# Expert weights stored as pieces of 128 rows of 2 KB instead of rows of 8 KB, in a gated cross-attention and mixture-of-experts kernel

## The chip, the core and the metric

The kernel runs on one core of one Trainium2 chip. A core has TensorE (PE in the profile, with its weight loads as PEld), VectorE (DVE), ScalarE (ACT), GpSimd (POOL) and SyncE (SP). SP computes nothing here: it issues DMAs, in the order of its program, and waits before each for what that DMA needs. POOL issues the indirect DMAs (gathers and scatters). All DMAs are carried out by the core's 16 DMA engines; those that SP issues appear in the profile as queue q1, those of POOL as q0, those of ACT as q10.

The metric is device time in microseconds, lower is better. The kernel before takes 445.69 us, the median of five runs from 444.35 to 446.97.

## The reference, cut to what matters

```python
x = x + jnp.tanh(g_xattn[0]) * xattn(layernorm(x), ctx_1024, itok, Wq, Wkv, Wo)
x = x + jnp.tanh(g_ffn[0])   * ffn(layernorm(x), gate_w, w1, b1, w2, b2)

# ffn: 8 experts, the best 2 per token
gate_probs = softmax(einsum('bsh,eh->bse', x, gate_w))
top_v, top_i = jax.lax.top_k(gate_probs, 2)
comb_w = einsum('bsk,bske->bse', top_v, one_hot(top_i, 8))
for e in range(8):
    h = silu(einsum('bsh,hf->bsf', x, w1[e]) + b1[e])     # w1[e]: 256 x 1024
    y = einsum('bsf,fh->bsh', h, w2[e]) + b2[e]           # w2[e]: 1024 x 256
    out = out + y * comb_w[..., e:e+1]
```

There are 4 x 512 = 2048 tokens of 256 channels, all in fp32. In the attention each token looks at four neighbouring rows of a key and value table (16 heads of 16); which rows is given by `itok`. One expert's `w1` is 1 MB, its `w2` too.

## The kernel before, in words

**Attention and routing.** The 2048 tokens are 16 tiles of 128. The key and value table is projected first and written to DRAM (`near`). For each tile POOL gathers its four table rows per token (L224, 1 MB), DVE does the scores and the weighted sum (L391 to L432), and PE the projections. Then tiles are routed in groups: DVE finds each token's two best experts and the place of the token in the expert's region of a DRAM table `xs`, and POOL scatters the normalised rows there (L331, two scatters for each tile). `queue` turns the counts so far into a list `blk` of blocks, each of 128 rows of one expert. The list is lengthened as tiles are done, and at the end eight scatters of a padding row (`xs<-padrow,pad`) fill the last rows.

**Blocks of the experts.** There are 39 of them. For block `s`, `fetch` lets SP read the expert's number and the block's first row into registers and issue five DMAs in this order: `w1s` (the expert's whole `w1`, 1 MB, L693), `xg` (the 128 rows, L697, which waits for the scatters that may write them), `b1s` (L699), `ms` (L702), `b2s` (L708). PE then turns the rows (`turn`, L714), multiplies them with `w1` (`up`, 32 matmuls, L729, with silu on ACT), and, one block later, with `w2` (`down`, 16 matmuls, L754). In PE's order: `up(s)`, `turn(s+1)`, `down(s-1)`. DVE forms the weighted result `yw` (L764), and POOL adds it into the output with an indirect accumulating DMA (L765).

**What sets the order.** Most buffers of a block are threefold (`ffn` pool). `b2s` of a block waits until DVE's `yw` three blocks earlier has read the old one; since SP goes in program order, the next block's `w1s` and `xg` are issued only after that. `w2` of all experts is loaded once: eight loads of 1 MB (L851), two behind each of the first four attention tiles.

**How the weights lie.** On the host, `by_row` puts each expert's weights in the order in which the partitions of SBUF want them: row `e*128 + p` of `w1` or `w2` is the 8 KB that partition `p` holds of expert `e`. So a load is 128 rows, each contiguous in DRAM and in SBUF:

```python
nc.sync.dma_start(
    out=w1s.rearrange("p k f -> p (k f)"), in_=w1[bass.ds(be_v * P, P), :]
)
```

Of the kernel before, what the change touches and what calls it, by code (L numbers as in the profile page):

```python
# [15 lines left out]

P = 128
KW = 4
EPS = 1e-5
FMAX = 3.4028234663852886e38  # L20

# [2 lines left out]
def gated_xattn_moe(  # L24
# [25 lines left out]
    nc = tc.nc  # L50
    NTOK, D = x.shape
    E = b2.shape[0]
    F = b1.shape[1] * P
    NT = NTOK // P
    KD = D // P
    NF = F // P
# [4 lines left out]
    GROUPS = [(sum(sizes[:i]), n) for i, n in enumerate(sizes)]  # L61
    EDGE = KW - 1
    LKW = LKV + 2 * EDGE
# [8 lines left out]
    @contextmanager  # L72
    def in_order():

        traced = nc.cur_bb.bb.instructions
        old = {i.name for i in traced}
        yield
        for i in nc.cur_bb.bb.instructions:
            if i.name not in old and i.engine == mybir.EngineType.DVE:
                if order:  # L80
                    tc.add_manual_dep(i, order[-1].name, ORDER, reason="in this order")
                order.append(i)
# [3 lines left out]
    def surely(tiles):  # L86

        return max(0, -((E * (P - 1) - TOPK * P * tiles) // P))
# [31 lines left out]
    for b in range(1, B):  # L120
        nc.sync.dma_start(
            out=src_rest[:, :, b - 1, :], in_=kvT[:, :, b * LKW + EDGE : b * LKW + EDGE + P]
        )
    gw_sb = const.tile([P, KD, E], F32, name="gw_sb")
    w2_sb = const.tile([P, E * NF, D], F32, name="w2_sb")
# [11 lines left out]
        out=upto,  # L137
        in_=all_one,
# [44 lines left out]
    nc.vector.tensor_copy(seg_f, seg_i)  # L183
    neg = const.tile([P, NT, KW], F32, name="neg")
    for o in range(KW):
        nc.vector.tensor_scalar(
            neg[:, :, KW - 1 - o], seg_f, float(o), -FMAX, ALU.is_lt, ALU.mult
        )
# [25 lines left out]
    def project_near(kv, psum, src, b, after=None):  # L214
        copy = nc.vector.tensor_copy if b == 0 else nc.scalar.copy
        project(kv, psum, src, P, near[b], EDGE, f"near{b}", copy, after)
        return nc.sync.dma_start(
            out=near[b][0:EDGE, :].unsqueeze(0),
            in_=kv[0:1, :].unsqueeze(1).to_broadcast([1, EDGE, 2 * D]),
        ).ins  # L220
# [23 lines left out]
    def rsqrt(pool, mv, rs, nm, n, name):  # L244
# [3 lines left out]
        g = nc.vector  # L248
        g.tensor_scalar(v, mv[:, :, 1], EPS, None, ALU.add)
        g.tensor_scalar(  # L250
# [48 lines left out]
    def layers(is_near):  # L299
        order.clear()  # L300
        with ExitStack() as inner:
            _layers(inner, is_near)

    def _layers(ctx, is_near):
# [36 lines left out]
        def reads_rows(i, done):  # L341

            for other in scatters[:done]:
                tc.add_manual_dep(i, other.name, SYNC, reason="rows of any scatter so far")
            for other in scatters[done:]:
                tc.declare_no_dep(i, other, reason="rows of their own")
            reads.append(i)
# [5 lines left out]
        def rows_of(t):  # L353
            gt = gat.tile([P, KW, 2 * D], F32, tag="g", name=f"g_{t}")
            if is_near:
                gather_near(gt, t)
            else:
                gather(gt, every, B * LKW, idx_every[:, t : t + 1])
            gathered[t] = gt
# [4 lines left out]
        def stage_in(t):  # L364

            xn = att.tile([P, D], F32, tag="xn", name=f"xn_{t}")
            normalise(xn, t, rsa[:, t : t + 1], nma[:, t : t + 1])
            px = ps_m.tile([P, KD, P], F32, tag="m", name=f"px_{t}")
            for k in range(KD):
                nc.tensor.transpose(px[:, k, :], xn[:, ts(k, P)], ident)  # L370
            xnT = att.tile([P, KD, P], F32, tag="xnT", name=f"xnT_{t}")
            nc.scalar.copy(xnT, px)
            ops[t] = xnT

        def stage_ask(t):

            xnT = ops.pop(t)
            pq = ps_q.tile([P, D], F32, tag="q", name=f"pq_{t}")
            for k in range(KD):
                nc.tensor.matmul(  # L380
                    pq, xnT[:, k, :], wq_sb[:, k, :], start=(k == 0), stop=(k == KD - 1)
                )
            ops[t] = pq

        def stage_attend(t):

            pq = ops.pop(t)
            gt = gathered.pop(t)
            prod = att.tile([P, KW, D], F32, tag="prod", name=f"prod_{t}")
            sc = small.tile([P, KW, H], F32, tag="sc", name=f"sc_{t}")  # L390
# [79 lines left out]
        def centre():  # L470
            pg = ps_m.tile([P, E], F32, tag="m", name="pg")
            for k in range(KD):
                nc.tensor.matmul(pg, all_one, gw_sb[:, k, :], start=(k == 0), stop=(k == KD - 1))
            nc.vector.scalar_tensor_tensor(
                gwc,
                pg.unsqueeze(1).to_broadcast([P, KD, E]),
                -1.0 / D,
                gw_sb,
                ALU.mult,
                ALU.add,  # L480
            )
# [195 lines left out]
        def fetch(s, blk, i):  # L677
            be_v = nc.values_load(  # L678
                blk[0:1, i, 0:1],
                engines=[SP],  # L680
                min_val=0,
                max_val=E - 1,
                skip_runtime_bounds_check_because=why,
            )
            br_v = nc.values_load(  # L685
                blk[0:1, i, 1:2],
                engines=[SP],
                min_val=0,
                max_val=E * CAP,
                skip_runtime_bounds_check_because=why,  # L690
            )
            w1s = ffn.tile([P, KD, F], F32, tag="w1s", name=f"w1s_{s}")
            nc.sync.dma_start(  # L693
                out=w1s.rearrange("p k f -> p (k f)"), in_=w1[bass.ds(be_v * P, P), :]
            )
            xg = ffn.tile([P, D], F32, tag="xg", name=f"xg_{s}")
            reads_rows(nc.sync.dma_start(out=xg, in_=xs[bass.ds(br_v, P), 0:D]).ins, done[s][0])  # L697
            b1s = ffn.tile([P, NF], F32, tag="b1s", name=f"b1s_{s}")
            nc.sync.dma_start(out=b1s, in_=b1[bass.ds(be_v * P, P), :])  # L699
            ms = ffn.tile([P, 2], F32, tag="ms", name=f"ms_{s}", bufs=6)  # L700
            reads_rows(
                nc.sync.dma_start(  # L702
                    out=ms, in_=xs[bass.ds(br_v, P), bass.ds(be_v * 2 + D, 2)]
                ).ins,
                done[s][0],
            )
            b2s = ffn.tile([P, D], F32, tag="b2s", name=f"b2s_{s}")
            nc.sync.dma_start(out=b2s, in_=b2[bass.ds(be_v, 1), :].to_broadcast([P, D]))  # L708
            return w1s, xg, b1s, ms, b2s
# [102 lines left out]
        for i in range(NT + 1):  # L812
            if i + AHEAD < NT:
                rows_of(i + AHEAD)
            if i + 1 < NT and i:
                stage_in(i + 1)
            attend = stage_attend(i) if i < NT else iter(())
            queued = surely(i) if i in ends else 0
            with in_order():
                if i != sizes[0] + sizes[1]:  # L820

                    next(attend, None)
                    next(attend, None)
                if i == 1:
                    centre()
                if i:
                    stage_out(i - 1)
                if i + 1 < NT:
                    stage_ask(i + 1)
                if i in ends and i > sizes[0]:  # L830
                    for _ in stage_route(ends[i]):
                        pass
                if i == NT:
                    queue(i, NS - before)
                elif queued:
                    queue(i, queued - before)
                    before = queued
                for _ in attend:
                    pass
                if i + 1 == sizes[0] + sizes[1]:  # L840
                    for _ in stage_route(0):
                        pass
            if is_near and i == 0:
                for b in range(1, B):
                    project_near(
                        kv_near[:, b, :], ps_m, src_rest[:, :, b - 1, :], b, after=exps[0]
                    )
            if i < E // 2:

                for e in (2 * i, 2 * i + 1):  # L850
                    load = nc.sync.dma_start(out=w2_sb[:, ts(e, NF), :], in_=w2[ts(e, P), :])  # L851
                    tc.add_manual_dep(load.ins, seen[i].name, SYNC, reason="after its rows")
        s = 0
        while s < NS:
# [79 lines left out]
```

## Time and profile before

| | |
|---|---|
| median of 5 runs | 445.69 us |
| the profiled execution | 447.19 us, with a span of 445.0 us in the profile |
| PE busy | 376.3 us (85% of the span) |
| DVE, ACT, POOL busy | 217.9, 174.0, 167.7 us |
| DMA | 94.76 MB in 43977 packets; q1 47.4% and q0 21.6% of 16 engines' span |
| DMAs that the change touches | `w1s` 39 of 1 MB, `w2_sb` 8 of 1 MB |

Up to some 82 us DVE does the attention of the first tiles while the gathers and the `w2` loads go on. From 82 to some 290 us the rest of the attention and the first half of the blocks share PE. From some 304 us PE has only blocks left, the last 17 of them in a steady rhythm.

How to read it: busy time alone does not tell what bounds the kernel. The lists of waits say for which engine's instruction or which DMA an engine stood idle, and for how long; the chain of work that ended last is followed back from the end. A DMA's landing time is counted from its issue to its completion as the waiting engines see it. In the DMA part, a queue's line gives packets, megabytes, and the time of its packets as a share of the 16 engines' span.

### The profile page before, as it was taken

How to read it: one execution, taken by the hardware profiler on the slowest of the kernel's cores; microseconds unless marked ns; L12 is line 12 of the kernel's file. 1: busy time of each engine (PE TensorE's matmuls, PEld its weight loads, DVE VectorE, ACT ScalarE, POOL GpSimd, SP SyncE). 2: the span in 40 equal slices, each digit the busy share in tenths (PEclk: the TensorE clock that was granted, in tenths of full speed). 3: DMA queues.
4: the chain of work that ended last, by engine and by line, in shares of the span. 5: the costliest groups of instructions: out<-in, count | busy, mean ns of one | idle time of the engine just before them, and what ended most of it. 6: DMA issues, size and time to landing. Idle time of an engine off the chain costs nothing. (4 is left out here: it accounts for less than half of the span.)

```text
span 445.0 us, 7747 instructions
## 1 busy us (share of the span) xinstructions
PE 376.3 (85%) x2311; PEld 330.9 (74%) x2311; DVE 217.9 (49%) x748; ACT 174.0 (39%) x476; POOL 167.7 (38%) x187
## 2 busy tenths in 40 slices
PE   1577755379999899599899899989999999999991
PEld 0235533268899788499889889878999999999980
DVE  1859996865987985664984954110111111111100
ACT  0322224127458467166557553323332424242320
POOL 4111124413472535323723627725342334242321
PEclk9996665569999999889999999999999999999996
DMA  6599993473976692695776966867767777786612
GB/s 204 180 355 388 423 393 131 158 251 143 300 217 234 217 292 47 223 340 160 243 195 169 257 161 187 260 176 207 235 165 230 182 212 185 210 216 181 150 16 27
DMA packets 43977, 94.76 MB, mean 213 GB/s; under 512 B 15756, under 2 KB 32524, under 8 KB 35864
## 3 DMA queue, kind: packets, MB, share of 16 engines
q1 hardware_dynamic: 33224, 65.66, 47.4%
q0 software_dynamic: 9840, 27.47, 21.6%
q10 hardware_dynamic: 864, 1.06, 0.7%
q8 instruction: 21, 0.34, 0.3%
q14 instruction: 28, 0.23, 0.2%
HBM read 80.17 MB, written 13.99 MB: 212 GB/s over the span
## 5 line engine op out<-in xcount | busy, mean ns | idle before, releaser
L729 PE MATMUL ph<-xgT,w1s 128*128 128x128 f32 x1248 | 152.1, 277 | 0.1
L729 PEld LDWEIGHTS ph<-xgT,w1s 128*128 128x128 f32 x1248 | 149.0, 193 | 2.5 <-DVE xgT L717 0.5
L754 PE MATMUL py<-w_sb,hT 128*128 x624 | 147.0, 383 | 2.0 <-DVE yw L764 0.7
L739 ACT ACTIVATE hT<-ph,b1s 128x128 f32<-128x128 f32 x312 | 88.0, 372 | 113.8 <-issue 90.0
L754 PEld LDWEIGHTS py<-w_sb,hT 128*128 128x128 f32 x624 | 114.4, 191 | 17.3 <-issue 4.1
L765 POOL DMA_INDIRECT out<-yw,ms x39 | 63.1, 1617 | 125.3 <-DMA out<-yw,ms 45.3
L763 POOL TENSOR_SCALAR b2s<-b2s,ms 128x256 f32<-128x256 f32 x39 | 42.4, 1087 | 50.1 <-DMA b2s<-in_b 49.1
L764 DVE SCALAR_TENSOR_TENSOR yw<-py,ms,b2s 128x256 f32<-128x256 f32 x39 | 18.8, 483 | 81.9 <-PE py L754 79.8
L717 DVE COPY xgT<-pxg 128x256 f32<-128x256 f32 x39 | 16.4, 420 | 86.0 <-PE pxg L714 86.0
L331 POOL DMA_INDIRECT xs<-rows,pos x32 | 33.6, 1051 | 27.3 <-DVE upb L619 6.5
L224 POOL DMA_INDIRECT g<-near,idx_near x16 | 18.1, 1131 | 50.1 <-DVE v L424 34.7
L714 PE MATMUL pxg<-ident,xg 128*128 128x128 f32 x78 | 15.7, 284 | 12.2 <-DMA xg<-xs 12.2
L380 PE MATMUL pq<-wq_sb,xnT 128*128 128x256 f32 x64 | 22.2, 479 | 3.8 <-DVE prod L391 3.8
L445 PE MATMUL po<-wo_sb,aoT 128*128 128x256 f32 x64 | 22.9, 492 | 2.8 <-ACT aoT L442 2.8
L739 ACT ACT_TABLE_LOAD x16 | 20.5, 1283 | 11.4 <-issue 9.8
L380 PEld LDWEIGHTS pq<-wq_sb,xnT 128*128 128x128 f32 x64 | 15.9, 251 | 8.9 <-DVE prod L391 4.7
L391 DVE TENSOR_TENSOR prod<-pq,g 128x1024 f32<-128x1024 f32 x16 | 19.5, 1217 | 4.9 <-PE pkv_near L206 4.9
L714 PEld LDWEIGHTS pxg<-ident,xg 128*128 128x128 f32 x78 | 9.8, 145 | 14.6 <-DMA xg<-xs 7.7
L424 DVE TENSOR_TENSOR v<-g,pr 128x1024 f32<-128x1024 f32 x16 | 19.9, 1242 | 0.5
L394 DVE TENSOR_REDUCE sc<-prod 128x64 f32<-128x1024 f32 x16 | 19.5, 1218 | 0.4
L445 PEld LDWEIGHTS po<-wo_sb,aoT 128*128 128x128 f32 x64 | 14.4, 241 | 7.0 <-ACT aoT L442 5.1
L442 ACT COPY aoT<-pa 128x256 f32<-128x256 f32 x16 | 6.0, 375 | 27.3 <-PE pa L440 27.1
(142 smaller groups left out, 314.0 us busy)
## 6 DMA issues: line engine op xcount, KB each, us to landing
w1s<-in_w SPq DMA_DIRECT2D x39, 1024.0 KB, 5.8
w_sb<-in_w SPq DMA_DIRECT2D x8, 1024.0 KB, 15.1
xg<-xs SPq DMA_DIRECT2D x39, 128.0 KB, 5.6
b2s<-in_b SPq DMA_DIRECT2D x39, 128.0 KB, 4.1
x_sb<-in_x SPq DMA_DIRECT2D x4, 512.0 KB
near<-kv_near SPq DMA_DIRECT2D x4, 256.0 KB, 3.8
out<-x_sb SPq DMA_DIRECT2D x4, 256.0 KB, 3.0
out<-x_sb SPq DMA_DIRECT2D x5, 128.0 KB
```

The source lines that it names most:

```text
L331: i = nc.gpsimd.indirect_dma_start(out=xs, out_offset=bass.IndirectOffsetOnAxis(ap=where, axis=0), in_=rows, in_offset=None,).ins
L380: nc.tensor.matmul(pq, xnT[:, k, :], wq_sb[:, k, :], start=(k == 0), stop=(k == KD - 1))
L391: seen[t] = nc.vector.tensor_tensor(prod, pq.unsqueeze(1).to_broadcast([P, KW, D]), gt[:, :, 0:D], ALU.mult).ins
L394: nc.vector.tensor_reduce(sc.rearrange("p o h -> p (o h)"), prod.rearrange("p o (h d) -> p (o h) d", d=HD), AX.X, ALU.add,)
L424: nc.vector.tensor_tensor(v.rearrange("p o (h d) -> p o h d", d=HD), gt[:, :, D : 2 * D].rearrange("p o (h d) -> p o h d", d=HD), pr.unsqu ...
L445: nc.tensor.matmul(po, aoT[:, k, :], wo_sb[:, k, :], start=(k == 0), stop=(k == KD - 1))
L714: nc.tensor.transpose(px[:, k, :], xg[:, ts(k, P)], ident)
L729: nc.tensor.matmul(ph[:, i, :], w1s[:, k, ts(f, P)], xgT[:, k, :], start=(k == 0), stop=(k == KD - 1),)
L739: nc.scalar.activation(hT[:, f, :], ph[:, i, :], AF.Silu, bias=b1s[:, f : f + 1])
L754: nc.tensor.matmul(py, hT[:, f, :], w2_sb[:, bass.ds(be_v * NF + f, 1), :].rearrange("p o d -> p (o d)"), start=(f == 0), stop=(f == NF - 1),)
L763: nc.gpsimd.tensor_scalar(b2s, b2s, ms[:, 0:1], None, ALU.mult)
L765: acc = nc.gpsimd.indirect_dma_start(out=out, out_offset=bass.IndirectOffsetOnAxis(ap=ms[:, 1:2].bitcast(I32), axis=0), in_=yw, in_offset= ...
```

## The change

Each expert's 128 rows of 8 KB are cut into four pieces: piece `c` holds the `c`-th 2 KB of each of the 128 rows, and lies in DRAM as 128 rows of 2 KB, 256 KB in all. The four pieces of an expert follow one another. A load still brings the same 1 MB to the same places in SBUF, but partition `p` now gets four separate rows of 2 KB, 256 KB apart. This holds for the 39 loads of `w1s` and the 8 of `w2_sb`. Nothing else is changed; the order of the instructions on PE, DVE, ACT, POOL and SP is the same, and so are their waits.

```diff
+PIECES = 4
...
             w1s = ffn.tile([P, KD, F], F32, tag="w1s", name=f"w1s_{s}")
             nc.sync.dma_start(
-                out=w1s.rearrange("p k f -> p (k f)"), in_=w1[bass.ds(be_v * P, P), :]
+                out=w1s.rearrange("p k (c f) -> p (k c) f", f=KD * F // PIECES),
+                in_=w1[bass.ds(be_v * (PIECES * P), PIECES * P), :].rearrange(
+                    "(c p) n -> p c n", p=P
+                ),
             )
...
-                    load = nc.sync.dma_start(out=w2_sb[:, ts(e, NF), :], in_=w2[ts(e, P), :])
+                    load = nc.sync.dma_start(
+                        out=w2_sb[:, ts(e, NF), :].rearrange(
+                            "p (c f) d -> p c (f d)", c=PIECES
+                        ),
+                        in_=w2[ts(e, PIECES * P), :].rearrange("(c p) n -> p c n", p=P),
+                    )
...
+    def in_pieces(w):
+        w = w.reshape(E, P, PIECES, -1)
+        return w.transpose(0, 2, 1, 3).reshape(E * PIECES * P, -1)
...
-        "w1": by_row(L0_ffn_w1),
+        "w1": in_pieces(by_row(L0_ffn_w1)),
...
-        "w2": by_row(L0_ffn_w2),
+        "w2": in_pieces(by_row(L0_ffn_w2)),
```

## The prediction

> **What bounds the kernel now.** I read the list of engines first, then the busy time by stretches, to see where PE has idle time at all; after that PE's waits, before and after 305 us.
>
> ```profile
> 304.00:431.00 127.00, 126.66 (x864) 118.88 (x864) 15.58 (x35) 39.25 (x138) 44.78 (x35) 1.00 0.70 185
> ```
>
> The columns are the stretch, its length, busy time of PE, PEld, DVE, ACT and POOL, the granted clock, the DMA share and GB/s. In the last stage PE is busy for 126.66 of 127 us at full clock, while the DMA engines are busy for 0.70 of the time. So the loads could be somewhat slower there at no cost, as long as each arrives in time. PE's waits from 84 to 305 us, then from 305 us to the end (us in total, times, longest):
>
> ```profile
> PE pxg L714 <- DMA xg<-xs: 12.2, 7, 5.6
> PE pa L440 <- DVE ao L432: 5.7, 5, 1.5
> ...
> PE py L754 <- DVE yw L764: 0.7, 1, 0.7
> ```
>
> PE never waits for `w1s` or `w2`, the loads that change. The DMA it waits for is `xg`, seven times, all before 305 us. Whether the change matters is therefore decided by what these loads do to other transfers: `xg` follows `w1s` in the same queue (q1), and the scatters that `xg` waits for run on q0 beside `w1s`.
>
> SP's issues in the last stage, and PE's turns:
>
> ```profile
> 309.32 0.33 SPq L693 DMA_DIRECT2D w1s<-in_w  x1
> 310.17 0.33 SPq L697 DMA_DIRECT2D xg<-xs  x1
> 315.66 0.33 SPq L708 DMA_DIRECT2D b2s<-in_b  x1
> 318.46 0.38 PE L714 MATMUL pxg<-ident,xg 128*128 128x128 f32 x2
> ```
>
> The rows asked for at 310.17 are turned at 318.46, 8.29 us later; the landing of `xg` has a median of 5.6 us. The margin is 2.7 us in each of the last 16 blocks, those fetched from 301 us on (the intervals there lie between 7.9 and 8.4). SP itself rests from 311.8 (`ms` issued) to 315.66, when `b2s` may go: 3.9 us to spare.
>
> **The change part by part.** *Time of the packets.* Two stretches give prices, one with hardly anything but `w2` in packets of 8 KB (43 to 44.5 us), and one with mostly the table writes in packets of 2 KB (33.5 to 35.5):
>
> ```profile
> q1 hardware_dynamic: 84, 0.61, 96.9%
> ...
> q1 hardware_dynamic: 347, 0.69, 91.2%
> ```
>
> The first is 0.969 x 1.5 us x 16 = 23.3 engine-us for 0.61 MB, or 38.1 ns per KB. The second is 0.912 x 2 x 16 = 29.2 for 0.69 MB, or 42.3 ns per KB, and it holds 48 packets of a few bytes too. The single packets recorded in the trace agree: the 8 KB ones have a median of 309 ns, the 256 packets of 2 KB that loads of ACT's queue brought from DRAM 84 ns. A load of 1 MB gives each engine 8 packets of 309 ns = 2.47 us now, and 32 of 84 ns = 2.69 us then: +0.22 us. Bounds: 4 x 77 ns, nothing gained or lost, below; above, the 53.8 ns per KB of q1 in the busy last stage (61.7% of 49 us for 8.99 MB), 110 ns a packet, which would be 3.5 us or +1.05 a load. That second row mixes in thousands of tiny packets, so I take +0.22.
>
> *The issue on SP.* An issue with one row per partition takes 0.33 us. The only loads with two rows per partition, `src_rest` (L121), take 0.56 to 0.61 us. Four rows cost +0.25 us if it is the extra dimension that costs, +0.75 if it is each extra row. The longest `w1s` issue now is 0.90 us (at 301.25), which shows that SP can be held back while the queue is full; 32 packets per engine fill it sooner. I take +0.25 to +0.75, and note that SP's 3.9 us of rest covers either.
>
> *The last 16 blocks.* `xg` lands later by 0.22, at worst by 1.05 + 0.75 = 1.8 us. The margin of 2.7 us covers both: nothing.
>
> *The eight `w2` loads.* 8 x 0.22 = 1.8 us more of transfer. They are issued from 27.8 to 50.5 us; the DMA engines are full until about 68.5 us, and the first use (L754) is at 101.10. Cover: 30 us. Behind them on SP stand the output stores (waiting for DVE anyway), and `w1s` of the first block at 82.65. Gathers share the engines here, but DVE never waits for a gather between 27 and 82 us. Nothing.
>
> *The seven waits for `xg`.* Three of them (at 100.30, 195.25 and 303.55 us, 0.26, 0.17 and 0.25 us long) follow a `w1s` directly, and PE has no margin: each grows by 0.22 us, or by 0.22 + 0.75 at worst where the issue shows as well. In these three the queue is still bringing `b2s` when `w1s` is issued, so the longer issue is hidden and I take 0.22: 3 x 0.22 = +0.7 us (bound 2.9).
>
> The other four (at 91.22, 185.71, 224.46 and 295.44 us; 5.56, 3.77, 0.61, 1.55) come from scatters that landed late. Their `w1s` was issued at least 6.4 us before `xg`. While it runs the scatters get nothing: from 176.4 to 179.4 us three scatters were issued, but the only queue with packets was
>
> ```profile
> q1 hardware_dynamic: 97, 0.79, 93.8%
> ```
>
> Now the scatters wait for 8 long packets per engine. If 32 short ones are served in one go as well, they wait 0.22 us longer each, +0.9 over the four. If the engines change over to q0 in between, scatters land sooner: the best is the 2.4 us that they take from 60 to 80 us, against 4.4 in the median and 7.8 for the padding at 285.18. That is worth 2.1 us at 91.22 and at 185.71 and the whole of 0.61 and 1.55: 6.4 us at most. Nothing in the trace shows which, and the two ends are far apart; the row nearest to it, the three microseconds without one scatter packet, says that a load is not interrupted. I take 0.
>
> **Sum:** +0.7 us on the profiled execution's 447.19 (span 445.0 and 2.2 around it). That execution lies 1.5 above the median of the runs, 445.69, so I add the 0.7 to the median: 446.4 us.
>
> **Two rules of the Trainium skill.** The change's own direction has a rule against it. "Perfetto Trace Analysis", DMA Optimizations, says that batching small transfers, its example being from 2 KB to 4 or 8 KB, can raise throughput dramatically. The rows above put the difference at 9 to 11%, and in stages where PE sets the pace; by the rule the loads would be the bound and the time clearly longer. On the scatters, "DMA: Bandwidth & Descriptors", Queues, rings and completion order, says that an engine goes round the queues packet by packet, where one packet may hold 9 to 17 descriptors. If 8 descriptors are such a unit, a load in 32 would be broken off one to three times, and the sum would go towards the 6.4 us gain. No row here shows how many descriptors are drained together.
>
> **The rivals.**
>
> *Faster: scatters slip in between the short packets.* For it: the scatters' landing of 4.4 us against 2.4 when no load runs. Against it: the load's bytes are the same, so what scatters gain they must take from it. Worked out: 0.7 - 6.4 = -5.7, or 440.0 us. From 180 to 210 us the mean granted clock is 0.89, after the wait of 3.77 us; if that wait shrinks so much that the clock does not fall, some 3.3 us (0.11 x 30) more.
>
> *Slower: the load takes longer than the turn allows, in each of the last blocks.* Place: `xg` behind `w1s` in q1. It decides from 2.7 us more per load, which is (2.47 + 2.7) / 32 = 161 ns for a packet of 2 KB, 1.9 times the 84. For it: packets of one partition now lie 256 KB apart, and no row shows such a read. Against it: even the mixed row gives 110. Past that point each 0.4 us costs 16 x 0.4 = 6.4 us: 452.8.
>
> *Slower by less: SP is held back when the queue is full.* `xg`, `b1s` and `ms` are then issued later in the mixed stage, where SP also issues stores and has no fixed rest. For it: the 0.90 us issue at 301.25, 0.57 over the usual. The three tight waits grow by 0.22 + 0.75 + 0.57 = 1.5 us each: +4.6, 450.3.
>
> *The loads change nothing that can be seen*, in packets or landing, since the queue could join adjacent rows: it would be the same 445.7. Rows 256 KB apart cannot be joined, so I fold this into the likeliest.
>
> **How the numbers follow.** Chances: likeliest 0.50 (own range 445.0 to 448.6, from nothing to the bound of 2.9 on the three waits), faster rival 0.20, load too slow 0.18, SP held back 0.12. The repeated runs lie within 0.3% of their median, and 0.5%, 2.2 us, is about what a measurement of this kernel can tell from no change. The likeliest gives 0.46 to within 0.5%, and 0.02 to each side. Faster: 0.20 + 0.02 = 0.22; same 0.46; slower 0.18 + 0.12 + 0.02 = 0.32. The range goes down to the faster rival at 440.0, which leaves out about half of it, and up to 452, past the held-back SP and just under the slow load's price, which leaves out about half of that: some 0.2 in all.
>
> **What the profile after would show.** Right: q1 with some 18,000 packets more (47 x 384), landing of `xg` in the last stage 5.7 to 6.5 us, still no wait for `xg` after 305 us, the three tight waits 0.2 to 0.3 longer, the `w1s` issue between 0.58 and 1.1 us. Wrong: a wait of PE for `xg` or `w1s` in the last stage, a period there above the present 7.25 us, or the waits at 91, 186 and 295 us clearly shorter or longer. The forecast fails if an order among the queues that I cannot see decides when scatters land.

## The result, and the profile after

The changed kernel takes 450.07 us against 447.3 us for the kernel before, medians of 52 and 94 runs: a ratio of 1.0060, with a 95% interval from 1.0044 to 1.0075. It is slower by 0.6%, or 2.7 us (2.0 to 3.4). The ratio leaves out the few executions that lie more than 1.5% above the fastest of their kernel. The forecast was 446.4 against 445.69, so +0.7 us; the time lies in the range. The sign of the sum was right, its size was a quarter of what came. The likeliest case of the forecast was a change within 0.5%; the ratio is just beyond that, and 0.5% lies inside its interval.

The two profiled executions do not show this difference: 447.36 us now (span 445.2), 447.19 before (445.0). One execution differs from the next of the same kernel by more than the effect, so the profile tells here what happened to single steps, and the repeated runs tell the sum.

From the DMA part of the page of the changed kernel, q1's packets, megabytes and share of 16 engines' span:

```profile
q1 hardware_dynamic: 51272, 65.66, 47.8%
```

q1 has 18,048 packets more than the 33,224 before, which is 47 x 384 exactly. They carry the same bytes, and the share of the engines' time rose only from 47.4 to 47.8%.

The busy time in the last stage (stretch, length, PE, PEld, DVE, ACT, POOL, granted clock, DMA share, GB/s):

```profile
304.00:431.00 127.00, 126.28 (x865) 118.55 (x863) 15.50 (x34) 38.88 (x136) 45.09 (x35) 1.00 0.69 184
```

PE's waits of the changed kernel from 84 to 305 us, then from 305 us to the end (us in total, times, longest):

```profile
PE pxg L718 <- DMA xg<-xs: 14.1, 7, 5.6
...
PE py L758 <- DVE yw L768: 0.7, 1, 0.7
```

PE is as busy in the last stage as it was (126.28 of 127 us), and it still waits there for no weights and no `xg`. What grew is the list's first row, `xg` before 305 us: 14.1 us in place of 12.2, again seven times. These are the seven turns (start, duration, then in brackets the idle time before), and ahead of them the three of the kernel before that the prediction called tight:

```profile
100.30 0.41 PE L714 MATMUL pxg<-ident,xg 128*128 128x128 f32 x2 [0.26 <-DMA xg<-xs]
195.25 0.44 PE L714 MATMUL pxg<-ident,xg 128*128 128x128 f32 x2 [0.17 <-DMA xg<-xs]
303.55 0.41 PE L714 MATMUL pxg<-ident,xg 128*128 128x128 f32 x2 [0.25 <-DMA xg<-xs]
...
89.93 0.69 PE L718 MATMUL pxg<-ident,xg 128*128 128x128 f32 x2 [5.63 <-DMA xg<-xs]
100.05 0.41 PE L718 MATMUL pxg<-ident,xg 128*128 128x128 f32 x2 [1.20 <-DMA xg<-xs]
185.38 0.66 PE L718 MATMUL pxg<-ident,xg 128*128 128x128 f32 x2 [3.92 <-DMA xg<-xs]
195.27 0.44 PE L718 MATMUL pxg<-ident,xg 128*128 128x128 f32 x2 [0.88 <-DMA xg<-xs]
224.39 0.44 PE L718 MATMUL pxg<-ident,xg 128*128 128x128 f32 x2 [0.51 <-DMA xg<-xs]
294.21 0.41 PE L718 MATMUL pxg<-ident,xg 128*128 128x128 f32 x2 [0.98 <-DMA xg<-xs]
303.04 0.41 PE L718 MATMUL pxg<-ident,xg 128*128 128x128 f32 x2 [1.00 <-DMA xg<-xs]
```

They are the same seven turns as before. The three tight ones (100, 195 and 303 us) went from 0.26, 0.17 and 0.25 us to 1.20, 0.88 and 1.00, together +2.4. The four behind late scatters went from 5.56, 3.77, 0.61 and 1.55 to 5.63, 3.92, 0.51 and 0.98, together -0.45. The 1.9 us do not appear in the span, mostly because the first turn came 1.3 us earlier in this execution than in the one before.

SP's issues in the last stage, and a turn:

```profile
308.82 0.38 SPq L694 DMA_DIRECT2D w1s<-in_w  x1
309.73 0.33 SPq L701 DMA_DIRECT2D xg<-xs  x1
315.15 0.33 SPq L712 DMA_DIRECT2D b2s<-in_b  x1
317.95 0.38 PE L718 MATMUL pxg<-ident,xg 128*128 128x128 f32 x2
```

The issue of the 512 packets takes 0.38 us in place of 0.33. The single packet records of the 16 loads in that stage give the time from a load's issue to the end of its last packet: 5.51 us in the median before, 5.77 now. The turns stay 7.24 to 7.25 us apart.

From 176.4 to 179.4 us two scatters were issued, at 176.40 and 178.41 (in the kernel before there were two as well, at 176.87 and 178.89; the prediction's third had begun at 175.57). All the packets that the DMA engines carried in these three microseconds:

```profile
q1 hardware_dynamic: 393, 0.80, 80.0%
```

q0 has not one, as in the same stretch of the kernel before. But that is not how loads and q0 always meet. From 190.4 to 193.9 us, while a `w1s` load runs, the packets of an output scatter (`out<-yw,ms`, rows of 1 KB on q0) come beside it in both kernels, first the kernel before, then the changed one:

```profile
q1 hardware_dynamic: 180, 1.07, 81.1%
q0 software_dynamic: 102, 0.10, 18.2%
...
q1 hardware_dynamic: 510, 0.99, 80.0%
q0 software_dynamic: 144, 0.13, 23.6%
```

And from 197 to 200 us of the changed kernel a gather (`g<-near`, rows of 8 KB on q0) runs beside the next `w1s` load, in rows of 2 KB, and takes most of the engines' time:

```profile
q0 software_dynamic: 124, 0.96, 77.1%
q1 hardware_dynamic: 153, 0.29, 25.5%
```

So a load is not always served in one go, neither in 8 packets per engine nor in 32. Taken in the order of the queue, the packet records give each load's own time. The twelfth load, issued near 190 us, takes 3.2 to 3.7 us from its first packet to its last in the four records with `w1` in rows of 8 KB and `xg` behind it (two of them from the experiments below), with 29 to 56 of the gather's 128 packets in that time. In the four with 2 KB it takes 5.3 to 5.4 us, with 111 to 124. The sixth load, which meets no q0 packet in any of the eight, takes 3.6 to 3.9 and 3.6 to 3.9 us.

What falls on the first trace is the rival in which the load gets too slow for the turn of the last stage. The rival in which scatters slip in keeps its mechanism and loses its gain: rows of q0 do pass beside the load's packets, but the four waits behind scatters lose only the 0.45 us above. The third, SP held back, would need long issues; they have a median of 0.38 us, with a longest of 0.93 against 0.90 before.

### The profile page after: what moved, and what is told of

It is laid out like the page before. It is cut to its first block, busy times and chain, and to the rows that moved or that the text cites. A ratio compares the mean times of both kernels' runs of the same rounds, so it can differ in the third digit from the quotient of the medians.

```text
span 445.2 us, 7747 instructions
## 1 busy us (share of the span) xinstructions
PE 374.8 (84%) x2311; PEld 330.0 (74%) x2311; DVE 217.8 (49%) x748; ACT 174.3 (39%) x476; POOL 166.2 (37%) x187
## 3 DMA queue, kind: packets, MB, share of 16 engines
q1 hardware_dynamic: 51272, 65.66, 47.8%
## 4 chain that ended last, share of the span: by engine, by line
PE 49%; DVE 22%; DMA 16%; issue 5%; ACT 3%; POOL 2%; SPq 2%; ACTq 0%; DVEq 0%; POOLq 0%
PE ph L733 21%; PE py L758 20%; DMA xs<-rows,pos 3%; DMA g<-near,idx_near 3%; DMA xg<-xs 3%; PE po L446 3%; DVE v L425 3%; DMA x_sb<-in_x 2%; PE pxg L718 2%; POOL xs L332 2%; DMA b2s<-in_b 1%; DVE sc L395 1%; DVE prod L392 1%; ACT hT L743 1%; DVE v L431 1%
## 5 line engine op out<-in xcount | busy, mean ns | idle before, releaser
L767 POOL TENSOR_SCALAR b2s<-b2s,ms 128x256 f32<-128x256 f32 x39 | 43.5, 1116 | 48.3 <-DMA b2s<-in_b 47.2
L718 PE MATMUL pxg<-ident,xg 128*128 128x128 f32 x78 | 15.7, 284 | 14.1 <-DMA xg<-xs 14.1
L446 PEld LDWEIGHTS po<-wo_sb,aoT 128*128 128x128 f32 x64 | 14.1, 235 | 6.8 <-ACT aoT L443 4.9
L441 PE MATMUL pa<-ident,ao 128*128 128x128 f32 x32 | 7.5, 320 | 10.8 <-DVE ao L433 10.8
```

The source lines that it names most:

```text
L446: nc.tensor.matmul(po, aoT[:, k, :], wo_sb[:, k, :], start=(k == 0), stop=(k == KD - 1))
L718: nc.tensor.transpose(px[:, k, :], xg[:, ts(k, P)], ident)
L767: nc.gpsimd.tensor_scalar(b2s, b2s, ms[:, 0:1], None, ALU.mult)
```

## The experiments

Two questions were open: which loads cost the time, and whether the waits for `xg` are the place. Theory A said that the 39 `w1` loads cost it, through `xg`, which stands behind a longer load where PE has no margin. Theory B, its rival, put it into the eight `w2` loads, in the stage in which the DMA engines are full. Theory C was any other cost of the `w1` loads, one that stays when `xg` no longer stands behind them. All ratios are to the kernel before on the same chip, with 95% intervals. The first and the third group of runs were on one chip (kernel before: 450.2 and 450.0 us), the second on another (447.6).

### One weight at a time

Only `w1` in pieces; against the changed kernel the edit puts `w2` back:

```diff
-    load = nc.sync.dma_start(out=w2_sb[...].rearrange("p (c f) d -> p c (f d)", c=PIECES), in_=...)
+    load = nc.sync.dma_start(out=w2_sb[:, ts(e, NF), :], in_=w2[ts(e, P), :])
...
-        "w2": in_pieces(by_row(L0_ffn_w2)),
+        "w2": by_row(L0_ffn_w2),
```

> Only the 39 w1 loads are in pieces, the eight w2 loads are rows of 8 KB as before. Theory A (the rows xg wait behind a longer w1 load, at three blocks without margin): the whole cost stays, ratio to the kernel before 1.004 to 1.008, and PE's waits for xg total 13.5 to 14.5 us against 12.2. Theory B (the w2 loads, in the stage where the DMA engines are full, delay the gathers or the stores): ratio 1.000 within 0.2%.

Measured: 451.72 us, 1.0031 (0.9994 to 1.0068). The waits for `xg` sum to 13.6 us. By itself this run does not tell the cost from none; it has to be read with the next two.

Only `w2` in pieces, which is the same edit on `w1s` and on `"w1"`:

```diff
-    out=w1s.rearrange("p k (c f) -> p (k c) f", f=KD * F // PIECES), in_=...
+    out=w1s.rearrange("p k f -> p (k f)"), in_=w1[bass.ds(be_v * P, P), :]
...
-        "w1": in_pieces(by_row(L0_ffn_w1)),
+        "w1": by_row(L0_ffn_w1),
```

> Only the eight w2 loads are in pieces. Theory A: nothing, ratio 0.998 to 1.002, PE's waits for xg as before at 12.2 us. Theory B: the whole cost, 1.004 to 1.008, with DVE or PE waiting in the first 90 us.

Measured: 449.45 us, 0.9995 (0.9956 to 1.0033). The time is that of the kernel before, which speaks against theory B. But the waits for `xg` sum to 13.7 us, not to the 12.2 of before, although `w1` was loaded as before: the tight waits at 97.64 and 196.09 us were 1.29 and 1.10 us long. So a tight wait of a microsecond is no sign of the pieces by itself, and my reading of the first pair of traces (+2.4 us in three waits) was too confident.

The third group repeated this with a larger dose: `w2` alone in pieces of 128 rows of 1 KB, eight packets for each one of before.

```diff
-PIECES = 4
+PIECES = 8
```

> Only the eight w2 loads in eight pieces of 1 KB rows, w1 in rows of 8 KB, the order of issue as before. Theory A: nothing, 0.998 to 1.002. Theory B (the w2 loads in the full stage cost): a good part of what eight pieces cost in both, 1.005 to 1.013.

Measured: 449.41 us, 0.9988 (0.996 to 1.0016). The `w2` loads cost nothing that can be measured even in 1 KB. Theory B is out, and what is left of the changed kernel's cost lies with the 39 loads of `w1s`.

### Packets or places

The 2 KB pieces of a partition lie beside each other, 2304 bytes apart, in place of 256 KB. The number and size of the packets are unchanged (`w2` is loaded in the same way; its lines are left out here):

```diff
-        w = w.reshape(E, P, PIECES, -1)
-        return w.transpose(0, 2, 1, 3).reshape(E * PIECES * P, -1)
+        w = w.reshape(E * P, PIECES, -1)
+        w = np.pad(w, ((0, 0), (0, 0), (0, 64)))
+        return w.reshape(E * P, -1)
...
-                in_=w1[bass.ds(be_v * (PIECES * P), PIECES * P), :].rearrange("(c p) n -> p c n", p=P),
+                in_=w1[bass.ds(be_v * P, P), :].rearrange("p (c n) -> p c n", c=PIECES)[
+                    :, :, 0 : KD * F // PIECES
+                ],
```

> All loads again in 512 packets of 2 KB, but a partition's four rows of 2 KB lie beside one another in DRAM, 2304 bytes apart (256 bytes of padding), not 256 KB apart. Theory A1 (the number of packets costs): the same as the changed kernel, ratio 1.004 to 1.008, the three tight waits of PE for xg 0.9 to 1.2 us each. Theory A2 (reading four places 256 KB apart costs): back to 0.999 to 1.002, the three waits at 0.2 to 0.5 us.

Measured: 451.74 us, 1.0030 (0.9998 to 1.0062), the waits for `xg` 14.5 us. It is the same ratio as with `w1` alone in far pieces, and not clear of the changed kernel's 1.0060 either, so nothing points to the distance; an effect of 0.3% or less could not be seen here. In the last stage the loads take 5.38 us in the median, no longer than rows of 8 KB, while the twelfth load beside the gather takes 5.4 us from its first packet, as with far pieces. The issue of `w1s` took 0.55 us in the median, longer than with far pieces, and the time did not follow it.

### The two kernels again, and 1 KB

On the second chip the kernel before ran as its own control.

> The kernel before, unchanged, as a control and for a second trace of it. Ratio 1.000 within its interval. The two tight waits of PE for xg near 98 and 196 us were 0.26 and 0.17 us in the first trace of this kernel, but 1.29 and 1.10 us in the trace of the kernel with pieces in w2 alone, whose w1 loads are the same as here. If they come out near 1.1 again, they differ from chip to chip, and a comparison of two traces says nothing on the change; near 0.2, the w2 pieces would have to be the cause.

Measured: 447.19 us, 1.0007 (0.9978 to 1.0037). Its turns that waited:

```profile
88.37 0.69 PE L714 MATMUL pxg<-ident,xg 128*128 128x128 f32 x2 [5.52 <-DMA xg<-xs]
97.78 0.41 PE L714 MATMUL pxg<-ident,xg 128*128 128x128 f32 x2 [0.49 <-DMA xg<-xs]
181.99 0.41 PE L714 MATMUL pxg<-ident,xg 128*128 128x128 f32 x2 [2.89 <-DMA xg<-xs]
191.61 0.44 PE L714 MATMUL pxg<-ident,xg 128*128 128x128 f32 x2 [1.36 <-DMA xg<-xs]
222.95 0.46 PE L714 MATMUL pxg<-ident,xg 128*128 128x128 f32 x2 [2.62 <-DMA xg<-xs]
294.70 0.41 PE L714 MATMUL pxg<-ident,xg 128*128 128x128 f32 x2 [1.44 <-DMA xg<-xs]
303.14 0.41 PE L714 MATMUL pxg<-ident,xg 128*128 128x128 f32 x2 [0.61 <-DMA xg<-xs]
```

They sum to 14.9 us, 2.8 more than in the first record of the same kernel. This is how much one record says of a sum of waits.

The changed kernel, unaltered:

> The changed kernel, unchanged, beside the control on one chip. Ratio 1.003 to 1.008. Theory A (rows xg behind a longer w1 load): the sum of PE's waits for xg is 1 to 3 us above that of the control's trace.

Measured: 450.34 us, 1.0084 (1.0049 to 1.012). Five of its nine waiting turns, whose waits sum to 17.6 us:

```profile
90.23 0.69 PE L718 MATMUL pxg<-ident,xg 128*128 128x128 f32 x2 [5.92 <-DMA xg<-xs]
99.85 0.41 PE L718 MATMUL pxg<-ident,xg 128*128 128x128 f32 x2 [1.24 <-DMA xg<-xs]
...
126.12 0.44 PE L718 MATMUL pxg<-ident,xg 128*128 128x128 f32 x2 [0.69 <-DMA xg<-xs]
186.90 0.66 PE L718 MATMUL pxg<-ident,xg 128*128 128x128 f32 x2 [4.45 <-DMA xg<-xs]
196.87 0.44 PE L718 MATMUL pxg<-ident,xg 128*128 128x128 f32 x2 [2.07 <-DMA xg<-xs]
```

The wait at 126.12 us, which no record of the kernel before has, stands behind the fifth load, which met a whole gather and took 10.8 us from its issue; with 8 KB it takes 6.2 to 7.2.

This execution is 4.4 us longer than that of the control (span 449.3 against 444.9), and 2.1 us of it lie behind the last `yw`. The last `yw` and the last output scatter of the control, then of the changed kernel:

```profile
434.86 0.48 DVE L764 SCALAR_TENSOR_TENSOR yw<-py,ms,b2s 128x256 f32<-128x256 f32 x1 [3.93 <-PE py L754]
436.39 1.56 POOL L765 DMA_INDIRECT out<-yw,ms  x1 [3.62 <-DMA out<-yw,ms]
...
437.09 0.48 DVE L768 SCALAR_TENSOR_TENSOR yw<-py,ms,b2s 128x256 f32<-128x256 f32 x1 [3.93 <-PE py L758]
440.82 1.56 POOL L769 DMA_INDIRECT out<-yw,ms  x1 [3.02 <-DMA out<-yw,ms]
```

Each output scatter waits for the one before it. Here POOL issues them 8 to 11 us behind their `yw` through most of the last stage, in the control 0.3 to 3 us after its first block, and at the end the backlog has to be worked off.

And with both weights in 1 KB rows, 1024 packets for each load (`PIECES = 8`):

> Eight pieces of 1 KB rows, 1024 packets to a load. By the trace of before a packet of 1 KB takes 46 ns, so an engine's share is 64 x 46 = 2.94 us against 2.69 for 2 KB and 2.47 for 8 KB. Theory A: the load is 0.47 us longer than before, twice as much as with 2 KB rows, so the three tight waits and with them the kernel lose about twice as much, ratio 1.008 to 1.016; still no wait for xg in the last stage. If the number of descriptors holds SP back in the last stage, a ratio of 1.03 or more.

Measured: 451.98 us, 1.0134 (1.0097 to 1.017). This lies above the interval of the changed kernel's main measurement (1.0044 to 1.0075), so the effect grows with the number of packets; the two intervals on this chip alone overlap. Three waiting turns, and two in a row of the last stage:

```profile
88.76 0.69 PE L718 MATMUL pxg<-ident,xg 128*128 128x128 f32 x2 [6.06 <-DMA xg<-xs]
98.35 0.41 PE L718 MATMUL pxg<-ident,xg 128*128 128x128 f32 x2 [0.70 <-DMA xg<-xs]
...
194.52 0.44 PE L718 MATMUL pxg<-ident,xg 128*128 128x128 f32 x2 [1.19 <-DMA xg<-xs]
...
320.54 0.38 PE L718 MATMUL pxg<-ident,xg 128*128 128x128 f32 x2
327.78 0.38 PE L718 MATMUL pxg<-ident,xg 128*128 128x128 f32 x2
```

The rows of `xg` and `b2s` are 1 KB too, so the records don't show where a load ends. `w1s` and `xg` together are through 6.1 us after the issue of `w1s`, in the median of the last stage; it is 6.1 and 6.2 us with 2 KB rows and 5.9 and 5.8 with 8 KB. So `xg` comes some 0.3 us later there, within the margin of 2.7 us, and PE still doesn't wait: the turns are 7.24 us apart. On the tight waits theory A was not borne out: with twice the packets, the waits at 98 and 194 us are not longer than those of 2 KB rows.

### Xg ahead of w1s

If the cost arises because `xg` stands behind `w1s`, it should go when `xg` is issued first. That can be done where no scatter is newer than the block before, which holds for 31 of the 39 blocks:

```diff
+            rows_first = s > 0 and done[s][0] == done[s - 1][0]
+            if rows_first:
+                xg = ffn.tile(...)
+                reads_rows(nc.sync.dma_start(out=xg, ...).ins, done[s][0])
             w1s = ffn.tile(...)
             nc.sync.dma_start(out=w1s..., in_=w1...)
-            xg = ffn.tile(...)
-            reads_rows(...)
+            if not rows_first:
+                xg = ffn.tile(...)
+                reads_rows(...)
```

First the changed kernel with this order:

> The changed kernel with one move: in a block whose rows are written by no scatter later than those of the block before, SP issues xg ahead of w1s; elsewhere the order stays. Theory A: the three tight waits of PE for xg (some 1.0 us each) go to nothing, PE's waits for xg total about 11 us, and the ratio to the kernel before falls to 0.998 to 1.002 or a little below. If something else costs (theory B, or other waits), the ratio stays at 1.004 to 1.008 although the three waits are gone.

Measured: 449.0 us, 0.9964 (0.9927 to 1.0). The order gains about as much as the pieces lose, or more; that alone doesn't say whether it takes away the pieces' own cost or one that rows of 8 KB have too.

Then, with the second group, the kernel before with it:

> The kernel before with rows of 8 KB, and xg issued ahead of w1s in blocks that need no scatter later than the block before. Theory A: the tight waits go (0.7 us in the first trace, some 2.4 where they are as long as in the last traces), ratio 0.994 to 0.999, and no slower than the changed kernel with the same move (0.9964).

Measured: 442.82 us, 0.9917 (0.9887 to 0.9947), faster than both kernels. The turns that still waited:

```profile
88.86 0.69 PE L719 MATMUL pxg<-ident,xg 128*128 128x128 f32 x2 [5.59 <-DMA xg<-xs]
182.68 0.41 PE L719 MATMUL pxg<-ident,xg 128*128 128x128 f32 x2 [3.83 <-DMA xg<-xs]
220.28 0.44 PE L719 MATMUL pxg<-ident,xg 128*128 128x128 f32 x2 [0.60 <-DMA xg<-xs]
290.45 0.41 PE L719 MATMUL pxg<-ident,xg 128*128 128x128 f32 x2 [1.29 <-DMA xg<-xs]
```

The three tight waits are gone, and the four behind scatters are left. `xg` lands after 3.1 us in the median, `w1s` after 7.2 (of those whose landing the record tells). So this order pays in rows of 8 KB too. It gains 3.7 us, more than the tight waits of the two records of the kernel before (0.7 and 2.5 us), so it takes away more than these waits.

To compare 8 KB, 2 KB and 1 KB in this order on one chip, the third group ran all three. Rows of 8 KB:

> The kernel before with xg issued ahead of w1s, once more, as the base for the next two. Ratio 0.989 to 0.995 as in the first run of it (0.9917).

Measured: 445.35 us, 0.9892 (0.9846 to 0.9939). Two of the three turns that waited, here and in the next two records; the third, near 223 us, waited 0.55, 0.68 and 0.80 us:

```profile
90.45 0.69 PE L719 MATMUL pxg<-ident,xg 128*128 128x128 f32 x2 [5.46 <-DMA xg<-xs]
184.05 0.66 PE L719 MATMUL pxg<-ident,xg 128*128 128x128 f32 x2 [3.75 <-DMA xg<-xs]
```

Rows of 2 KB:

> The changed kernel with xg issued ahead of w1s, on one chip with the run above. Theory A (the pieces cost only because xg waits behind the longer load): the ratio is within 0.2% of the run above, 0.990 to 0.996. Theory C (the pieces cost elsewhere as well): it stays 0.4 to 0.8% above it, as the changed kernel stands to the kernel before.

Measured: 448.33 us, 0.995 (0.992 to 0.998).

```profile
89.42 0.69 PE L723 MATMUL pxg<-ident,xg 128*128 128x128 f32 x2 [5.77 <-DMA xg<-xs]
184.77 0.66 PE L723 MATMUL pxg<-ident,xg 128*128 128x128 f32 x2 [4.36 <-DMA xg<-xs]
```

Rows of 1 KB:

> Eight pieces of 1 KB rows, 1024 packets to a load, with xg issued ahead of w1s. Without the move eight pieces gave 1.0134. Theory A: within 0.4% of the first run of this call, some 0.990 to 0.998. Theory C: 1.0 to 1.3% above it, 1.001 to 1.008.

Measured: 449.55 us, 0.9994 (0.9969 to 1.002).

```profile
91.01 0.69 PE L723 MATMUL pxg<-ident,xg 128*128 128x128 f32 x2 [5.98 <-DMA xg<-xs]
186.09 0.66 PE L723 MATMUL pxg<-ident,xg 128*128 128x128 f32 x2 [4.11 <-DMA xg<-xs]
```

With the tight waits gone in all three, 1 KB still costs 1.0% (0.9994 - 0.9892; 0.5 to 1.6 if the two half-widths are added in squares), so theory A alone doesn't carry the effect, and there is a part of the kind that theory C named. For 2 KB the difference is 0.6%, with an interval from about 0 to 1.1, which leaves open whether all of the cost stays or hardly any.

One caution on this group. All records of its chip hold a stall that those of the other chip and the first pair lack. One of DVE's copies of the turned rows in the record of 2 KB rows with `xg` first (idle time in brackets):

```profile
283.93 0.42 DVE L726 COPY xgT<-pxg 128x256 f32<-128x256 f32 x1 [9.96 <-remote]
```

The turn before this copy had started at 277.46 us and takes 0.38, so the copy began some 6 us after its input was there. PE then had nothing to do, and the clock fell. PE's `up` after the stall, in PE's timeline (the one before it, at 273.79 us, took 3.84 us):

```profile
284.45 6.66 PE L738 MATMUL ph<-xgT,w1s 128*128 128x128 f32 x32 [3.15 <-issue]
```

The stretch from 282 us in the same record (columns as above, PEclk is the third number from the end):

```profile
282.00:292.00 10.00, 7.55 (x38) 7.50 (x39) 1.33 (x3) 3.12 (x12) 6.66 (x6) 0.66 0.56 168
```

The same stretch in the record of rows of 8 KB with `xg` first, where the stall was shorter and the clock stayed up:

```profile
282.00:292.00 10.00, 7.24 (x47) 6.52 (x48) 1.33 (x3) 3.43 (x12) 6.59 (x7) 1.00 0.62 171
```

From the turn before the stall to the one after it, two blocks took 19.2 us there and 21.8 with 2 KB rows (20.7 with 1 KB), where they take 14.5 in the changed kernel's record, which has no stall. The stall occurs with both layouts of `w1` (also in the two kernels with only `w2` changed), so it is not the pieces of `w1` that cause it. It differs between these records by up to 2.7 us, about as much as their kernels' times do, and whether it is longer on average with pieces no record of one execution can say.

## Why the prediction was right or wrong

**Time of the packets: right where a load runs alone.** The step said +0.22 us a load. In the last stage a load takes 5.51 and 5.43 us in the two records of the kernel before, 5.77 and 5.73 in the two of the changed one: +0.28. The sixth load, without q0, is 0.22 longer in the means of four and four. But over the 23 loads ahead of that, in the stage that they share with q0, the times from issue to last packet sum to 143 to 149 us with 8 KB (four records) and 153 to 160 with 2 KB: +0.41 a load in the mean, and +1.7 for the twelfth. The rule of the Trainium skill that the prediction weighed against this row ("Perfetto Trace Analysis", DMA Optimizations: larger transfers can raise throughput dramatically, named there for kernels that are bound by DMA) has the sign right. Here the loss was 0.6% of the time and 0.4 points of q1's share in the first pair, since the DMA engines are not what PE waits for in most of the kernel.

**The issue on SP: over-sized.** +0.25 to +0.75 us were taken, 0.05 was measured. The step cost nothing, as foretold.

**The last 16 blocks: right, and tested harder.** Behind the third tight wait (303 to 306 us) there is no wait for `xg` at 2 KB, nor at 1 KB. One foretold sign was wrong: `xg`'s landing in that stage was to be 5.7 to 6.5 us. The second record of the changed kernel tells two landings there, of 5.1 and 5.8 us, against 5.5 and 5.6 in the first of the kernel before.

**The eight `w2` loads: right.** 0.9995 and, in 1 KB rows, 0.9988.

**The three tight waits: the place was right, the size wrong.** "I take 0.22: 3 x 0.22 = +0.7 us (bound 2.9)". Taken over the records with `xg` behind `w1s`, four with `w1` in 8 KB rows and four with it in 2 KB, the wait near 100 us has a mean of 0.63 us (0.26 to 1.29) and 1.39 (1.20 to 1.77), that near 195 us 0.82 (0.17 to 1.36) and 1.20 (0.75 to 2.07). The wait near 303 us, which the records with the stall at 282 us do not have, has 0.43 (mean of two) and 1.15 (two). Together +1.9 us, within the bound, though the records overlap. The term that was too small is the 0.22 us a load: the step priced the load as if alone, and in that stage it shares the engines with output scatters and gathers. The three loads ahead of these `xg` take, from issue to last packet, 7.5, 8.1 and 6.8 us with 8 KB and 7.8, 8.6 and 8.4 with 2 KB (means of four and four records, for the third of the two and two without the stall): +0.3, +0.5 and +1.6, where the waits grew by 0.8, 0.4 and 0.7. What these loads meet explains why 0.22 was too little, not each wait's size.

**The four waits behind scatters: the value was right and then not taken.** The step worked out that each wait grows by 0.22 us if a load in 32 packets is served in one go, "+0.9 over the four", and then said "I take 0". Its ground, that a load is not interrupted, holds for the three microseconds it was read from and not elsewhere in the same trace, as the 102 packets of q0 from 190.4 to 193.9 us show. The first load of all, near 82 us, does meet no q0 packet, in any of the eight records. The first of the four waits, the cleanest of all, has the step's own size: 5.44 to 5.59 us in six records with `w1` in rows of 8 KB (mean 5.52), 5.63 to 5.92 in five with 2 KB (mean 5.76), 6.06 and 5.98 with 1 KB. That is +0.24 and +0.50. The second also grows, from 3.96 to 4.33 in the means of the same four and four records. The third jumps between 0.5 to 0.8 and 2.2 to 2.8 us in both layouts, so the sum of the four is beyond what these records can give.

**The rule on packets.** "DMA: Bandwidth & Descriptors", Queues, rings and completion order, of the Trainium skill says that an engine goes round the queues by packets, of 9 to 17 descriptors typically. The prediction feared that 32 short rows would be broken off that way. This case shows both: 393 packets of q1 and none of q0 from 176.4 to 179.4 us, with two scatters issued, and q0 and q1 side by side at 190 and at 197 us. Whether the scatters' packets were ready in the queue in the first stretch, no record tells, and none shows how many descriptors go at a turn. The gain that the prediction tied to it, up to 6.4 us through earlier scatters, did not come: in the records without the stall the four waits behind scatters sum to 11.5 and 12.5 us in the kernel before, to 11.0 and 12.0 in the changed one.

**The sum.** 0.7 us were foretold and 2.7 measured, near the upper end of the likeliest case (from nothing to 2.9). That 450.07 us stands beside the 450.3 of the rival with SP held back is chance: the kernel before is 1.6 us slower over 94 runs than over the five that the forecast added to. The tight waits (+1.9) and the first scatter wait (+0.2) are the part of PE's waits that was seen. Another part can sit at the end, which the prediction left out: from the last `yw` to the end of the span the four records with 8 KB take 9.2 to 9.6 us, the four with 2 KB 9.5, 9.9, 9.9 and 11.7, that with 1 KB 10.9. The rest isn't located, nor how these parts add up: the waits of one layout sum to 10.4 to 13.7 us up to 230 us from one record to the next, so the means over four cannot resolve a microsecond. What the pieces cost with `xg` first (1.0% at 1 KB) shows that there is more than the tight waits. Whether it sits in the waits behind scatters, in the clock after them, or in the length of the stall on that chip stays open; the end of the span it is not, which takes 10.3 to 10.5 us in that order with all three row lengths.

## What to carry to other kernels

Shorter rows cost little where the DMA engines have room in each block: rows that came 0.3 us later were free in a stage with 2.7 us of margin. So look for the few places without margin and price the change there, in the traffic of that stage and not by the load alone: beside a gather in rows of 8 KB, a load in rows of 2 KB took 2.0 us longer, not 0.2. When a step rests on a condition such as "a load is not interrupted", look for it in more than one stretch of the trace. And a small transfer that an engine waits for goes ahead of the large one in its queue: this was worth 0.8% (0.9917, 0.9887 to 0.9947) and again 1.1% (0.9892, 0.9846 to 0.9939), more than the change itself lost.

## What the runs showed of the hardware

- 512 packets of 2 KB are issued by SP in 0.38 us, 1024 of 1 KB in 0.38, 128 of 8 KB in 0.33; with the pieces 2304 bytes apart it took 0.55 us in the median. The number of rows does not set the issue time.
- In the single packet records a 2 KB packet of these loads takes 84 ns in the median and 98.5 in the mean, an 8 KB one 309 and 387, or 96.8 for each 2 KB. Over a whole run the cost per byte is nearly the same.
- Loads of q1 and transfers of q0 run side by side on the DMA engines in some stretches, and the load's share is smaller there with shorter rows. In the stretches of 0.25 us between 84 and 300 us in which both moved at least 80 GB/s, a load in rows of 8 KB moved 194 to 226 GB/s beside a gather's 178 to 205 (four records), a load in rows of 2 KB 155 to 165 beside 222 to 251 (four records).
- One chip's records all hold a stall between 272 and 290 us in which DVE's and ACT's instructions start some 5 to 6 us after their input is there, with both layouts, and the kernel before is 2.5 us slower on that chip. Its cause was not found.
- After PE's idle time of 3.15 us in that stall, 32 matmuls took 6.66 us in place of 3.73 to 3.84; after 1.97 us, in the record of rows of 8 KB with `xg` first, the granted clock stayed at 1.00.
